# One Strassen product of the query projection split again into seven, and quadrant 3's value matmuls joined in both batches

## The chip, the core and the metric

The kernel runs on one core of a Trainium2 chip. A core has five engines with a queue of instructions each: TensorE (PE, matrix products, with its weight loads shown apart as PEld), VectorE (DVE), ScalarE (ACT), GpSimd (POOL) and SyncE (SP, which issues the DMAs). Matmuls write to PSUM, which DVE and ACT read; everything else lies in SBUF. The metric is the device time of the one core in microseconds (us), lower is better. The times shown are of executions without the profiler, except where "the profiled execution" is named.

## What is computed

`x` holds 64 batches of 128 tokens of 512 features. It is normalised, and goes through an attention with 16 query heads of 64 that share one key and one value head, with a bias per head and a causal and a key mask; the result is projected, normalised and added to `x`:

```python
xn = layernorm(x, g_in)
q = (xn @ Wq).reshape(b, n, H, DH).transpose(0, 2, 1, 3) * scale
k, v = split(xn @ Wkv)                     # one head; a null key and value in front
attn = softmax(q @ k^T + bias, masked)     # causal, and mask per key
out = (attn @ v).transpose(0, 2, 1, 3).reshape(b, n, INNER) @ Wo
return x + layernorm(out, g_out)
```

All is in 32-bit floats. `xn @ Wq` is 512 by 512 by 1024 for each group of four batches.

## The kernel before

**Tiles and loop.** The batches are worked on in groups of four (`GB`), and in steps `d` of two batches `a = 2d` and `b = 2d + 1`. A step is `turn(d)` followed by `body(d)`, for `d` from 1 to 29; `turn_end` and `body_end` do the last two, and a start-up part stands before. There is no scheduler: the order in which the functions issue their instructions is the order on each engine (`manual_schedule`), so whatever stands at the head of an engine's queue and waits holds up all that is behind it.

**A turn.** It issues the scores of batches `a` and `b` (L616), has DVE add them to bias and mask (L631, L633), and does the values of the pair before, `p = 2d - 2` and `p + 1` (`values`, L745). A values matmul uses 32 rows and 64 columns of the array. For each of four row quadrants `s` and two halves `r` a batch takes a matmul of 256 columns and three of 128; `wide` names quadrants in which two of those three, with the same weights, are joined into one of 256. Before the change quadrant 3 is joined in the first batch `p` of even steps, and nowhere else.

**The query projection.** For group `g = d//2 + 1`, one of the two halves `h = d % 2` of its features is made in a step. `[features x 512] @ [512 x tokens]` is done by Strassen's scheme (Winograd's form): seven products of half size instead of eight. `a11 ... a22` are quarters of `wq` (`a12`: the upper 256 input features, the lower half of the outputs), `s1, s2, s4, s3` sums of them made once, and `token_sum` makes four sums `xS` of the tokens on POOL, in even steps for both steps of a group. `product(g, f, k, ...)` (L539) is product `k` for output chunk `f` of 128: two matmuls of 128 by 128 weights and 256 columns. A step does chunks `f0 = 2h` and `f1 = 2h + 1`. Results collect in three kinds of PSUM tiles: "a" and "c", one buffer each, and "w", two buffers. `keep` copies a state of "a" to SBUF on ACT (`kp1`, `ku2`, `ku3`; one buffer for each name); `q_out` adds a PSUM tile and a kept one into the query tile `qT` on DVE (L560), or copies on ACT (L557). Product 5 opens a "c" tile and product 3 closes it; `q_out(.., "c", "u3")` reads it between these, and `q_out(.., "c", "u2")` after product 3. The next product 5 can open "c" only after that second read. Product 2 has a "w" tile for itself, and `q_out(g, f, 0, "w", "p1")` adds it to `kp1`.

**Order of a body on PE** (numbers are query products, of chunk f0, then f1; o1 ... o7 the output projection's products by the same scheme, L831): key and value products (L353), 1, 2, o1, 5, 6, o2, 7 of f0; 2 of f1; 4, 3 of f0; 1, 5 of f1; o5; 6 of f1; o6; 7; o3; 3; o7; 4; o4.

**Order on DVE between products 7 and 5:** `q_out(.., "c", "u3")`, the second batch's gain (`pair_gain`, L892) and residual (`pair_residual`, L895) of the output's normalisation, a transposition of new tokens (`tokens_T(m)`, L325), `q_out(.., "c", "u2")`, and the second `tokens_T`. The two transpositions are issued while there is a group after next (`xw`), up to step 27.

Of the kernel before, what the change touches and what calls it, by code (L numbers as in the profile page):

```python
# [8 lines left out]
FP = mybir.dt.float32  # L9
U8 = mybir.dt.uint8  # L10
AF = mybir.ActivationFunctionType
ALU = mybir.AluOpType
# [5 lines left out]
def kernel(  # L18
# [86 lines left out]
    const = ctx.enter_context(tc.tile_pool(name="const", bufs=1))  # L105
# [344 lines left out]
    xS, prod, kept = {}, {}, {}  # L450
# [11 lines left out]
    def q_part(g, c, h):  # L462

        return qT[g, c % NF, h][:, :, :, c // NF, :]
# [58 lines left out]
    def product(g, f, k, pool, tag, start=True):  # L523

        if start:
            prod[tag] = pool.tile([P, HT], FP, tag=tag, name=f"p{tag}_{g}_{f}_{k}")
        lo, hi = xT[g][:, 0 : GB // 2], xT[g][:, GB // 2 :]
        t1, t2, t3, t4 = (xS.get((g, i)) for i in range(1, 5))
        w, t = {
            1: (a11, lo[:, :, lo_k]),  # L530
            2: (a12, lo[:, :, hi_k]),
            3: (s4, hi[:, :, hi_k]),
            4: (a22, t4),
            5: (s1, t1),
            6: (s2, t2),
            7: (s3, t3),
        }[k]
        for kc in range(HK):
            nc.tensor.matmul(  # L539
                prod[tag],  # L540
                w[:, kc, f * P : (f + 1) * P],
                t[:, :, kc, :],
                start=(start and kc == 0),
                stop=(kc == HK - 1),
                skip_group_check=not start,
            )

    def keep(tag, name, slot=None):
        slot = slot or name
        kept[name] = bp.tile([P, HT], FP, tag=f"k{slot}", name=f"k{name}", bufs=1)  # L550
        nc.scalar.copy(kept[name], prod[tag])  # L551

    def q_out(g, c, h, tag, name=None):
        o = q_part(g, c, h)
        p = prod[tag].rearrange("p (t h i) -> p t h i", t=2, h=2)
        if name is None:
            nc.scalar.copy(o, p)  # L557
        else:
            k = kept.pop(name).rearrange("p (t h i) -> p t h i", t=2, h=2)
            nc.vector.tensor_tensor(o, p, k, ALU.add)  # L560


    S, nmax, rsum = {}, {}, {}

    def mask_neg(g):
# [159 lines left out]
    def values(b, wide=()):  # L725

        g, t = divmod(b, GB)
        sb = sbs.pop(b)
        po = pos[b]
        turns = (  # L730
            ((0, 0, 2), (1, 1, 1), (2, 1, 1), (3, 1, 1)),
            ((0, 0, 2), (1, 0, 1), (1, 1, 1), (2, 1, 1)),
        )
        for turn in range(len(turns[0])):
            for s in range(NQ):
                j, to, n = turns[s % 2][turn]
# [50 lines left out]
    P_LAST = B - 2  # L787
    lo_e, hi_e = slice(0, HE), slice(HE, DIM)
    lo_c, hi_c = slice(0, HC), slice(HC, NC)
    wT = const.tile([P, 4, HC, HE], FP, name="wT")  # L790
    e11, e12 = wo[:, lo_c, lo_e], wo[:, lo_c, hi_e]
    e21, e22 = wo[:, hi_c, lo_e], wo[:, hi_c, hi_e]
    yS = {}

    def out_weight_sum(k):
        p, m = ((e12, e11), (e22, wT[:, 0]), (e22, e12), (e21, wT[:, 1]))[k]
        nc.gpsimd.tensor_tensor(wT[:, k], p, m, ALU.subtract)

    def out_sum(p, k, eng=nc.gpsimd):

# [12 lines left out]
    def out_product(p, k, pool, tag, start=True):  # L813
        key = "y" + tag
        if start and pool is ps_s:
            two = ps_s.tile([P, 2, DIM], FP, tag="s", name=f"py_{p}_{k}_s")
            prod[key] = two[:, 0, 0:HE]
        elif start:
            prod[key] = pool.tile([P, HE], FP, tag=tag, name=f"py{tag}_{p}_{k}")
        a, b = oT[p], oT[p + 1]  # L820
        h, w = {
            1: (a[:, 0], e11),
            2: (a[:, 1], e21),
            3: (a[:, 1], e22),
            4: (b[:, 1], wT[:, 3]),
            5: (yS.get(p), wT[:, 0]),
            6: (a[:, 0], wT[:, 1]),
            7: (b[:, 0], wT[:, 2]),
        }[k]
        for c in range(HC):  # L830
            nc.tensor.matmul(  # L831
                prod[key],
                h[:, c, :],
                w[:, c, :],
                start=(start and c == 0),
                stop=(c == HC - 1),
                skip_group_check=not start,
            )
# [35 lines left out]
    def pair_pow(b):  # L874
        nc.gpsimd.tensor_tensor(yn[b][1], yn[b][1], nhalf, ALU.pow)
# [43 lines left out]
    def turn(d):  # L919

        a, b, p = 2 * d, 2 * d + 1, 2 * d - 2
        g = d // 2 + 1
        homes = (ps_y, "Y"), (ps_q, "a")
        if d == 1:
            homes = homes[::-1]
        scores(a, 0, (homes[0], (ps_w, "w")))
        scores(b, 0, (homes[1], (ps_w, "w")))
        scores(a, 1)
        scores(b, 1, ((ps_y, "X"), (ps_q, "c")))
        scores_add(a, 0)  # L930
        scores_add(b, 0)
        scores_max(a, 0)
        scores_add(a, 1)
        scores_add(b, 1)
        po = values_rooms(p)
        values(p, () if d % 2 else (3,))
        values(p + 1)
        if d % 2 and (d + 1) // 2 < NG:
            mask_neg((d + 1) // 2)
        bias_add(a + 2)  # L940
        if d % 2 == 0:
            token_sum(g, 1)
            token_sum(g, 2)
        exps(a, 0)
        values_out(p, po)
# [262 lines left out]
    def body(d):  # L1208
# [6 lines left out]
        m = (g + 1) * GB + 2 * h  # L1215
        sums = q and h == 0 and d > 0
        f0, f1 = 2 * h, 2 * h + 1

        if q:
            tags = [q_tags[g - 1, f, h] for f in range(NF)]  # L1220
# [6 lines left out]
        if ln:  # L1227
            pair_stats(l + 1)
            pair_pow(l + 1)
        if q:  # L1230
            kv_pair_out(g * GB + 2 * h, pkv)
            if h == 1:
                keys_T(g)
                values_spread(g)
# [12 lines left out]
            keep("a", "p1")  # L1247
        if ln:
            pair_norm(l)
        if q:  # L1250
            product(g, f0, 2, ps_w, "w")
            q_out(g, f0, 0, "w", "p1")
        if soft:
# [40 lines left out]
        if q:  # L1294
            product(g, f0, 7, ps_q, "a", start=False)
            keep("a", "u3")
            q_out(g, HC + f0, 1, "c", "u3")
        if ln:
            pair_gain(l + 1)
            pair_residual(l + 1)  # L1300
            store(l + 1)
# [2 lines left out]
            tokens_T(m)  # L1304
        if soft:
            exps(a, 1, 0, 1)
        if q:
            product(g, f1, 2, ps_w, "w")
            product(g, f0, 4, ps_q, "a", start=False)
            q_out(g, HC + f0, 0, "a")  # L1310
            product(g, f0, 3, ps_q, "c", start=False)
            q_out(g, f0, 1, "c", "u2")
# [14 lines left out]
        if q:  # L1327
            product(g, f1, 1, ps_q, "a")
            keep("a", "p1")
            q_out(g, f1, 0, "w", "p1")  # L1330
        if soft:
            exps(a, 1, 4)
# [10 lines left out]
        if q:  # L1343
            product(g, f1, 6, ps_q, "a", start=False)
            keep("a", "u2")
        if soft:
            exps(b, 1, 3)
            blocks_T(a)
# [29 lines left out]
        if out:  # L1378
            out_product(p, 4, ps_y, "X", start=False)
            out_part(p + 1, 0, "X")  # L1380

    def gains_T():
        pg = ps_y.tile([P, KC], FP, tag="X", name="pg")
# [177 lines left out]
```

## Time and profile before

| what | value |
|---|---|
| time, median of 3 executions | 1034.14 us (1033.25 to 1034.31) |
| the profiled execution's own time | 1033.72 us |
| its span, first to last instruction | 1031.9 us |
| two steps in the middle, 15 (odd, from 500.74 us) and 16 (even, from 532.19 us) | 31.45 and 31.48 us |

The profiled execution is one run of the program with the hardware profiler. Each matmul in 32-bit floats shows as two records on PE and two weight loads on PEld, so a product of two matmuls has four records. Rows of the timeline give the start in us, the time, the engine and line, the tiles (out<-in), the shape, the count of merged instructions, and in brackets the idle time before with what ended it. The duration of a record reaches to the end of its last write; the next instruction on the engine can start before that.

### The profile page before, as it was taken

How to read it: one execution, taken by the hardware profiler on the slowest of the kernel's cores; microseconds unless marked ns; L12 is line 12 of the kernel's file. 1: busy time of each engine (PE TensorE's matmuls, PEld its weight loads, DVE VectorE, ACT ScalarE, POOL GpSimd, SP SyncE). 2: the span in 40 equal slices, each digit the busy share in tenths (PEclk: the TensorE clock that was granted, in tenths of full speed). 3: DMA queues.
4: the chain of work that ended last, by engine and by line, in shares of the span. 5: the costliest groups of instructions: out<-in, count | busy, mean ns of one | idle time of the engine just before them, and what ended most of it. 6: DMA issues, size and time to landing. Idle time of an engine off the chain costs nothing.

```text
span 1031.9 us, 31175 instructions
## 1 busy us (share of the span) xinstructions
PE 1022.9 (99%) x12339; PEld 902.7 (87%) x12339; DVE 770.3 (75%) x1630; ACT 680.4 (66%) x2709; POOL 724.1 (70%) x537
## 2 busy tenths in 40 slices
PE   9999999999999999999999999999999999999997
PEld 8888888888888888888888888888888888888886
DVE  6877777876777877678777778777787777777597
ACT  4756667666677566686666776666776667856582
POOL 4997767676775867758667676676767677585676
PEclk9999999999999999999999999999999999999999
DMA  7514152241613325143151521415223161331311
GB/s 222 165 33 140 63 171 77 74 117 64 182 68 104 96 63 177 63 124 107 42 168 63 159 81 52 148 63 175 75 94 106 57 183 62 104 81 35 93 63 63
DMA packets 69226, 105.12 MB, mean 102 GB/s; under 512 B 9044, under 2 KB 33496, under 8 KB 67288
## 3 DMA queue, kind: packets, MB, share of 16 engines
q1 hardware_dynamic: 68784, 102.73, 31.8%
q8 instruction: 97, 1.59, 0.6%
q14 instruction: 49, 0.40, 0.1%
q10 hardware_dynamic: 296, 0.40, 0.1%
HBM read 67.45 MB, written 35.65 MB: 100 GB/s over the span
## 4 chain that ended last, share of the span: by engine, by line
PE 96%; DVE 2%; POOL 1%; issue 1%; DMA 0%; ACT 0%; POOLq 0%; DVEq 0%; ACTq 0%
PE pa L539 20%; PE pyX L831 19%; PE pyY L831 10%; PE pc L539 10%; PE po L745 7%; PE pkv L353 6%; PE pyw L831 5%; PE pw L539 5%; PE pq L474 3%; PE ps L616 3%; PE sc_X L616 2%; PE sc_Y L616 2%; PE py_s L831 1%; PE sc_a L616 1%; PE sc_w L616 1%; DVE sb L685 1%
## 5 line engine op out<-in xcount | busy, mean ns | idle before, releaser
L647 ACT ACTIVATE s<-s,nmax 128x65 f32<-128x65 f32 (+1 forms) x1024 | 372.0, 367 | 62.0 <-DVE nmax L638 62.0
L669 POOL TENSOR_TENSOR s<-s,rinv 128x512 f32<-128x512 f32 (+1 forms) x132 | 190.7, 1447 | 166.6 <-DVE rinv L665 166.6
L581 POOL TENSOR_TENSOR s<-biasp,mneg 128x1552 f32<-128x1552 f32 (+1 forms) x65 | 206.0, 3172 | 41.2 <-DVE s L631 32.8
L647 ACT ACTIVATION_READ_ACCUMULATOR s<-s,nmax 128x1 f32 x1024 | 194.3, 190 | 0.0
L831 PE MATMUL pyX<-wT,oT 128*128 128x256 f32 x696 | 164.4, 379 | 0.0
L685 DVE STREAM_TRANSPOSE sb<-s 128x1536 f32<-128x1536 f32 (+1 forms) x68 | 113.8, 1677 | 58.5 <-POOL s L669 58.5
L831 PEld LDWEIGHTS pyX<-wT,oT 128*128 128x128 f32 x696 | 132.1, 190 | 18.1
L638 DVE TENSOR_REDUCE nmax<-s 128x8 f32<-128x1032 f32 (+1 forms) x128 | 121.5, 950 | 0.1
L539 PE MATMUL pa<-xS,wq 128*128 128x256 f32 x472 | 121.2, 379 | 0.0
L557 ACT COPY qT<-pa 128x256 f32<-128x256 f32 x59 | 22.0, 373 | 147.1 <-PE pa L539 147.0
L539 PEld LDWEIGHTS pa<-xS,wq 128*128 128x128 f32 x472 | 89.4, 190 | 12.5 <-issue 0.2
L280 POOL TENSOR_TENSOR rstd<-rstd,nhalf 128x1 f32<-128x1 f32 x64 | 35.5, 555 | 74.1 <-DVE rstd L279 71.6
L811 POOL TENSOR_TENSOR oT<-oT 128x512 f32<-128x512 f32 x64 | 80.6, 1277 | 3.8 <-PE pyw L831 1.5
L745 PE MATMUL po<-sb,vr 32*64 32x256 f32 (+1 forms) x4008 | 81.8, 303 | 0.0
L745 PEld LDWEIGHTS po<-sb,vr 32*64 32x64 f32 x4008 | 71.4, 130 | 8.3 <-issue 5.7
L560 DVE TENSOR_TENSOR qT<-pc,ku 128x256 f32<-128x256 f32 x118 | 49.1, 416 | 39.5 <-ACT ku L551 22.4
L764 ACT ACTIVATE oT<-po,nv 128x512 f32<-128x512 f32 (+1 forms) x127 | 73.8, 656 | 0.2
L551 ACT COPY ku<-pa 128x256 f32<-128x256 f32 x118 | 43.9, 372 | 41.3 <-PE pa L539 38.1
L353 PE MATMUL pkv<-wkv,xT 128*128 128x128 f32 x512 | 65.6, 281 | 0.1
L353 PEld LDWEIGHTS pkv<-wkv,xT 128*128 128x128 f32 x512 | 59.7, 191 | 5.4 <-DVE s L631 4.8
L539 PE MATMUL pw<-xT,wq 128*128 128x256 f32 x240 | 61.4, 379 | 0.0
L539 PE MATMUL pa<-xT,wq 128*128 128x256 f32 x236 | 60.6, 379 | 0.0
(167 smaller groups left out, 2256.3 us busy)
## 6 DMA issues: line engine op xcount, KB each, us to landing
res<-in_x_dram SPq DMA_DIRECT2D x64, 256.0 KB, 2.9
x<-in_x_dram SPq DMA_DIRECT2D x63, 256.0 KB, 4.5
out_dram<-y SPq DMA_DIRECT2D x63, 256.0 KB, 2.3
xd<-xb SPq DMA_DIRECT2D x14, 1024.0 KB
xT<-xd SPq DMA_DIRECT2D x56, 256.0 KB, 5.9
vr<-vd SPq DMA_DIRECT2D x64, 128.0 KB, 2.7
kT<-kd SPq DMA_DIRECT2D x64, 64.0 KB, 2.1
wo<-in_L_cond_Wo_dram SPq DMA_DIRECT2D x1, 2048.0 KB, 13.5
```

Of the source, the lines that this page charges most:

```text
L353: nc.tensor.matmul(pkv, xT[g][:, t, kc, :], wkv[:, kc, :], start=(kc == 0), stop=(kc == KC - 1),)
L539: nc.tensor.matmul(prod[tag], w[:, kc, f * P : (f + 1) * P], t[:, :, kc, :], start=(start and kc == 0), stop=(kc == HK - 1), skip_group_ch ...
L581: nc.gpsimd.tensor_tensor(S[b][:, :, keys], biasp[:, :, keys], mneg[:, t, keys] .unsqueeze(1) .broadcast_to([P, R8, keys.stop - keys.start ...
L616: nc.tensor.matmul(home[r][u * DH : (u + 1) * DH, f, :], qT[g, f, t // 2][rows, t % 2, hf, u], kT[g][rows, 0 : nk // Q, t, :], start=True, ...
L638: nc.vector.tensor_reduce(nmax[b][:, hf], S[b][:, :, WITH_NULL[hf]], AX.X, ALU.max, negate=True)
L647: nc.scalar.activation(row, row, AF.Exp, bias=nmax[b][:, hf, k : k + 1], accum_out=rsum[b][:, hf, k : k + 1],)
L669: nc.gpsimd.tensor_tensor(sv, sv, rinvs[b, hf][:, lo:hi].unsqueeze(2).broadcast_to([P, hi - lo, sv.shape[2]]), ALU.mult,)
L685: nc.vector.transpose(sbs[b][:, :, lo:hi].rearrange("p j e q -> p e j q"), S[b][:, lo:hi, 1 : ROW - 1].rearrange("p e (j k) -> p e j k", k=Q),
L745: nc.tensor.matmul(po[s][rows, to : to + n], vr[g][quad, j, t, :], sb[quad, slots, r * NF : (r + 1) * NF, :], start=(turn == 0), stop=True ...
L764: nc.scalar.activation(to, src, AF.Identity, bias=nv2)
L811: eng.tensor_tensor(o, a, b, op)
L831: nc.tensor.matmul(prod[key], h[:, c, :], w[:, c, :], start=(start and c == 0), stop=(c == HC - 1), skip_group_check=not start,)
```

## The change

- Product 2, `a12` times the upper features of the first two batches, is itself split into two by two by two blocks of 128 and done by the same scheme in seven matmuls of 128 columns (`inner_product`), for both chunks `f0` and `f1` together, where before there were two for f0 and two for f1, of 256 columns. This holds for steps 2 to 29 (`deep`); step 1 goes as before.
- The seven lie in one "w" tile with four places of 128 columns. Matmul 1 stands where product 2 of f0 stood; 6, 5 and 2 stand after product 7 of f0; product 2 of f1, which came next, is gone; 7 stands after product 1 of f1; 4 and 3 after product 6 of f1.
- Two additions of 256 columns on DVE (`q_out(.., "w", "p1")`) become seven of 128 (`inner_out`). One stands where the first stood; two stand around `q_out(g, HC + f0, 1, "c", "u3")`; two where the second stood; two before `blocks_T(a)`.
- POOL makes the token sums (`token_sums_inner`, three subtractions of 256, 128 and 128 columns) in even steps after `pair_pow(l + 1)`. DVE makes the weight sums (`weight_sums_inner`, four of 256 columns) once, at the end of step 1.
- Quadrant 3's values are joined in both batches of every step from 2 on.
- For room, the output projection's third weight sum replaces `e12` in place, so that `wT` has three parts instead of four; one warm-up matmul is dropped (`keep_busy(7)`).

```diff
+    wL = const.tile([P, 3, 2, P], FP, name="wL")
+    in_four = a12.rearrange("p k (h f m) -> p k f h m", h=2, f=2)
+    d11, d12 = in_four[:, 0, 0], in_four[:, 1, 0]
+    d21, d22 = in_four[:, 0, 1], in_four[:, 1, 1]
+    r1, r2, r4 = (wL[:, i] for i in range(3))
+    r3 = d21
+    def weight_sums_inner():
+        for o, p, m, op in (
+            (r1, d21, d22, ALU.add),
+            (r2, r1, d11, ALU.subtract),
+            (r4, d12, r2, ALU.subtract),
+            (r3, d11, d21, ALU.subtract),
+        ):
+            nc.vector.tensor_tensor(o, p, m, op)
+    def token_sums_inner(g):
+        x = gp.tile([P, 4, N], FP, tag="xL", name=f"xL_{g}", bufs=1)
+        lo = xT[g][:, 0 : GB // 2]
+        nc.gpsimd.tensor_tensor(x[:, 0:2], lo[:, 1, hi_k], lo[:, :, HK], ALU.subtract)
+        nc.gpsimd.tensor_tensor(x[:, 2], lo[:, 1, KC - 1], x[:, 0], ALU.subtract)
+        nc.gpsimd.tensor_tensor(x[:, 3], lo[:, 0, KC - 1], x[:, 2], ALU.subtract)
+        xL[g] = x
+    def inner_product(g, h, k):
+        if k == 1:
+            inner[g, h] = ps_w.tile([P, 4, N], FP, tag="w", name=f"pl_{g}_{h}")
...
+        w, t, at = {
+            1: (d11, lo[:, 0, HK], 0),
+            2: (d12, lo[:, 0, KC - 1], 2),
+            3: (r4, lo[:, 1, KC - 1], 1),
+            4: (d22, t4, 0),
+            5: (r1, t1, 1),
+            6: (r2, t2, 0),
+            7: (r3, t3, 0),
+        }[k]
+        nc.tensor.matmul(
+            inner[g, h][:, at],
+            w[:, h],
+            t,
+            start=k == 1,
+            stop=True,
+            skip_group_check=k != 1,
+        )
+    def inner_out(g, h, f, t, at, name=None):
+        o = q_part(g, 2 * h + f, 0)[:, t]
+        p = inner[g, h][:, at].rearrange("p (h i) -> p h i", h=2)
+        k = o
+        if name is not None:
+            k = kept[name].rearrange("p (t h i) -> p t h i", t=2, h=2)[:, t]
+        nc.vector.tensor_tensor(o, p, k, ALU.add)
...
-        values(p, () if d % 2 else (3,))
-        values(p + 1)
+        values(p, () if d == 1 else (3,))
+        values(p + 1, () if d == 1 else (3,))
...
+        deep = q and d > 1
...
+        if sums:
+            token_sums_inner(g)
...
-        if q:
+        if deep:
+            inner_product(g, h, 1)
+            inner_out(g, h, 0, 0, 0, "p1")
+        elif q:
             product(g, f0, 2, ps_w, "w")
             q_out(g, f0, 0, "w", "p1")
...
         if q:
             product(g, f0, 7, ps_q, "a", start=False)
             keep("a", "u3")
+        if deep:
+            for k in (6, 5, 2):
+                inner_product(g, h, k)
+            inner_out(g, h, 0, 1, 0, "p1")
+        if q:
             q_out(g, HC + f0, 1, "c", "u3")
+        if deep:
+            inner_out(g, h, 0, 0, 2)
...
+        if q and not deep:
+            product(g, f1, 2, ps_w, "w")
         if q:
-            product(g, f1, 2, ps_w, "w")
             product(g, f0, 4, ps_q, "a", start=False)
             q_out(g, HC + f0, 0, "a")
             product(g, f0, 3, ps_q, "c", start=False)
             q_out(g, f0, 1, "c", "u2")
...
             product(g, f1, 1, ps_q, "a")
             keep("a", "p1")
+        if deep:
+            inner_product(g, h, 7)
+            inner_out(g, h, 1, 1, 0, "p1")
+            inner_out(g, h, 1, 1, 1)
+        elif q:
             q_out(g, f1, 0, "w", "p1")
...
             product(g, f1, 6, ps_q, "a", start=False)
             keep("a", "u2")
+        if deep:
+            inner_product(g, h, 4)
+            inner_product(g, h, 3)
+            inner_out(g, h, 1, 0, 0, "p1")
+            inner_out(g, h, 0, 1, 1)
...
+        if d == 1:
+            weight_sums_inner()
...
-    keep_busy(8)
+    keep_busy(7)
```

More of the change, by code (lines that the diff above doesn't have):

```diff
@@ L560, in q_out @@
             nc.vector.tensor_tensor(o, p, k, ALU.add)
+    wL = const.tile([P, 3, 2, P], FP, name="wL")
[4 more added lines that the diff above has]
+    r3 = d21
+    xL, inner = {}, {}
+    def weight_sums_inner():
[16 more added lines that the diff above has]
+            inner[g, h] = ps_w.tile([P, 4, N], FP, tag="w", name=f"pl_{g}_{h}")
+        lo = xT[g][:, 0 : GB // 2]
+        x = xL.get(g)
+        t1, t3, t2, t4 = (x if x is None else x[:, i] for i in range(4))
+        w, t, at = {
[22 more added lines that the diff above has]
+        nc.vector.tensor_tensor(o, p, k, ALU.add)
     S, nmax, rsum = {}, {}, {}
@@ L789 @@
     lo_c, hi_c = slice(0, HC), slice(HC, NC)
-    wT = const.tile([P, 4, HC, HE], FP, name="wT")
+    wT = const.tile([P, 3, HC, HE], FP, name="wT")
     e11, e12 = wo[:, lo_c, lo_e], wo[:, lo_c, hi_e]
     e21, e22 = wo[:, hi_c, lo_e], wo[:, hi_c, hi_e]
+    sums_e = wT[:, 0], wT[:, 1], e12, wT[:, 2]
     yS = {}
     def out_weight_sum(k):
-        p, m = ((e12, e11), (e22, wT[:, 0]), (e22, e12), (e21, wT[:, 1]))[k]
-        nc.gpsimd.tensor_tensor(wT[:, k], p, m, ALU.subtract)
+        p, m = ((e12, e11), (e22, sums_e[0]), (e22, e12), (e21, sums_e[1]))[k]
+        nc.gpsimd.tensor_tensor(sums_e[k], p, m, ALU.subtract)
     def out_sum(p, k, eng=nc.gpsimd):
@@ L824, in out_product @@
             3: (a[:, 1], e22),
[L825 to L828, printed above, removed]
+            4: (b[:, 1], sums_e[3]),
+            5: (yS.get(p), sums_e[0]),
+            6: (a[:, 0], sums_e[1]),
+            7: (b[:, 0], sums_e[2]),
         }[k]
```

## The prediction

> **What bounds the kernel now.** I read the page first: busy shares, and the chain that ended last.
>
> ```profile
> PE 1022.9 (99%) x12339; PEld 902.7 (87%) x12339; DVE 770.3 (75%) x1630; ACT 680.4 (66%) x2709; POOL 724.1 (70%) x537
> PE 96%; DVE 2%; POOL 1%; issue 1%; DMA 0%; ACT 0%; POOLq 0%; DVEq 0%; ACTq 0%
> ```
>
> PE is never without work. So matmul time taken out is a gain only if nothing else becomes late, and any wait that PE gets is a loss. Next the stage table, for steps 15 and 16 (span, then busy time of PE, PEld, DVE, ACT, POOL):
>
> ```profile
> 500.74:532.19 31.45, 31.45 (x386) 27.78 (x385) 23.86 (x51) 21.75 (x85) 19.71 (x15) 1.00 0.48 140
> 532.19:563.67 31.48, 31.48 (x382) 27.80 (x381) 23.52 (x50) 20.72 (x83) 24.02 (x18) 1.00 0.19 66
> ```
>
> Averages hide where DVE is tight, so I went through step 15 in the timeline, PE first:
>
> ```profile
> 506.03 2.05 PE L353 MATMUL pkv<-wkv,xT 128*128 128x128 f32 x16
> 507.92 1.03 PE L539 MATMUL pa<-xT,wq 128*128 128x256 f32 x4
> 508.79 1.03 PE L539 MATMUL pw<-xT,wq 128*128 128x256 f32 x4
> 509.65 1.89 PE L831 MATMUL pyX<-wo,oT 128*128 128x256 f32 x8
> 511.38 1.03 PE L539 MATMUL pc<-xS,wS 128*128 128x256 f32 x4
> 512.24 1.03 PE L539 MATMUL pa<-xS,wS 128*128 128x256 f32 x4
> 513.10 1.89 PE L831 MATMUL pyw<-wo,oT 128*128 128x256 f32 x8
> 514.83 1.03 PE L539 MATMUL pa<-xS,wq 128*128 128x256 f32 x4
> 515.69 1.03 PE L539 MATMUL pw<-xT,wq 128*128 128x256 f32 x4
> 516.56 1.03 PE L539 MATMUL pa<-xS,wq 128*128 128x256 f32 x4
> 517.42 1.03 PE L539 MATMUL pc<-xT,wS 128*128 128x256 f32 x4
> 518.28 1.03 PE L539 MATMUL pa<-xT,wq 128*128 128x256 f32 x4
> 519.15 1.03 PE L539 MATMUL pc<-xS,wS 128*128 128x256 f32 x4
> ```
>
> These are, from 507.92: products 1 and 2 of f0, o1, 5, 6, o2, 7 of f0 (514.83), 2 of f1 (515.69), 4 and 3 of f0, then 1 (518.28) and 5 (519.15) of f1. A product starts 0.863 us after the one before, 0.216 a record. The place to look at is product 5 of f1, which opens a new "c" tile. Weight loads, DVE and ACT around it:
>
> ```profile
> 517.21 0.84 PEld L539 LDWEIGHTS pc<-xT,wS 128*128 128x128 f32 x4
> 518.07 0.84 PEld L539 LDWEIGHTS pa<-xT,wq 128*128 128x128 f32 x4
> 519.03 0.73 PEld L539 LDWEIGHTS pc<-xS,wS 128*128 128x128 f32 x4
> ```
> ```profile
> 515.45 0.37 DVE L861 TENSOR_TENSOR y<-pyw,kyp 128x256 f32<-128x256 f32 x1
> 516.30 0.42 DVE L560 TENSOR_TENSOR qT<-pc,ku 128x256 f32<-128x256 f32 x1 [0.47 <-ACT ku L551]
> 516.64 0.69 DVE L892 TENSOR_TENSOR yn<-yn,gob 128x512 f32<-128x512 f32 x1
> 517.36 0.69 DVE L895 TENSOR_TENSOR y<-yn,res 128x512 f32<-128x512 f32 x1
> 517.97 0.70 DVE L325 STREAM_TRANSPOSE xb<-x 128x512 f32<-128x512 f32 x1
> 518.60 0.39 DVE L560 TENSOR_TENSOR qT<-pc,ku 128x256 f32<-128x256 f32 x1
> ```
> ```profile
> 515.89 0.37 ACT L551 COPY ku<-pa 128x256 f32<-128x256 f32 x1 [0.84 <-PE pa L539]
> ```
>
> Weight loads come 0.86 apart (517.21, 518.07), so the next was due at 518.93; it came at 519.03, 0.04 after the second `q_out` from "c" ended on DVE (518.60 + 0.39 = 518.99). The matmul followed at 519.15, just on time. **This hand-over has no slack left**, though no idle time shows. The chain behind it: product 7 of f0, ACT's copy, `q_out(.., "c", "u3")` at 516.30, gain, residual and transposition without a gap, `q_out(.., "c", "u2")` at 518.60: 2.30 us from the first `q_out` to the second.
>
> **The change part by part.** The rows for small matmuls and small additions:
>
> ```profile
> L353 PE MATMUL pkv<-wkv,xT 128*128 128x128 f32 x512 | 65.6, 281 | 0.1
> L399 DVE TENSOR_TENSOR kvt<-pkv,nkv 128x256 f32<-128x256 f32 x31 | 13.2, 424 | 19.1 <-PE pkv L353 19.1
> L388 DVE TENSOR_TENSOR kvt<-pkv,nkv 128x128 f32<-128x128 f32 x2 | 0.5, 281 | 0.0
> ```
>
> *Matmuls.* The key and value products, 16 records of 128 columns, take from 506.03 to 507.92: 1.89 us, 0.118 a record, more than half of 0.216. Seven inner matmuls are 14 records, 1.65 us; the four taken out are 1.73. By itself that saves 0.075 us a step, 2.1 us in 28 steps. The shape is the same as in that row, so I take it; at half of 0.216 a record the saving would be 0.215 a step, 6.0 in all.
>
> [...]
>
> *Where PE then stands.* Matmul 1 (0.236) in place of product 2 of f0 brings all that follows forward by 0.627: product 7 of f0 to 514.20. Matmuls 6, 5, 2 (0.708) follow from 515.07 to 515.77. Products 4, 3 of f0 and 1 of f1 (2.59) and matmul 7 (0.236) follow, and product 5 of f1 is due at 518.60, 0.55 earlier than now. Matmuls 4 and 3 (0.472) come behind it.
>
> *Where DVE then stands.* In the built program `inner_out(g, h, 0, 1, 0, "p1")` stands ahead of `q_out(.., "c", "u3")` and waits for the third of matmuls 6, 5, 2. Its last record starts at 515.65 and ends 0.28 later, 515.93; DVE follows a PE group by 0.04:
>
> ```profile
> 508.12 0.42 DVE L399 TENSOR_TENSOR kvt<-pkv,nkv 128x256 f32<-128x256 f32 x1 [0.59 <-PE pkv L353]
> ```
>
> (that group ended at 506.03 + 2.05 = 508.08). So it starts at 515.97, when DVE has long done the addition at 515.45. Additions of 256 columns start 0.34 apart (516.30 to 516.64) at a duration of 0.42; one of 128 is 0.14 shorter by the rows above (424 and 281), so 0.20 apart. Then: `inner_out` 0.20, `q_out` 0.34, the second `inner_out` 0.20, gain, residual and transposition 1.96 (516.64 to 518.60): the second `q_out` starts at 518.67, ends at 519.06, and the matmul follows 0.16 after that (518.99 to 519.15): **519.22**. PE was due at 518.60: it waits 0.62 us, with 0.05 of that taken earlier at product 4 (ACT's copy) and 0.13 at product 3 (which needs the first `q_out`), all inside the same total. Behind product 5 nothing is shorter, and matmuls 4 and 3 add 0.472. So a step grows by 0.07 + 0.47 = **0.54 us**, instead of shrinking by 0.075.
>
> [...]
>
> Bounds for the price of 128 columns in DVE's queue: 0.34 each, the same as 256 (+0.28 on the chain), or nothing (then the second `q_out` starts at 518.27 and PE still waits 0.22, a step growing by 0.14). I take 0.20, from the nearest row.
>
> The wait repeats while the transposition stands in the chain: steps 2 to 27, 26 times, 14.0 us. In steps 28 and 29 the chain is shorter by 0.63 and I count the saving of 0.075 each.
>
> *Values.* Value stages without a join (step 15) and with one (step 16):
>
> ```profile
> 503.58:506.03 2.45, 2.45 (x128) 2.20 (x128) 1.00 0.03 7
> 535.03:537.51 2.48, 2.48 (x124) 2.23 (x124) 1.00 0.21 78
> ```
>
> The one with a join has four records fewer and takes 0.03 us longer. No row shows both batches joined. Bounds per step: as much again for each (+0.06 odd, +0.03 even), or a gain of the mean share of the records left out (8 of 128 in 2.45: 0.15). I take 2.48 for both: +0.4 us in all; bounds -3.8 to +1.3.
>
> *The rest.* POOL's token sums:
>
> ```profile
> 535.06 1.27 POOL L521 TENSOR_TENSOR xS<-xT 128x512 f32<-128x512 f32 x1
> 541.35 0.55 POOL L280 TENSOR_TENSOR rstd<-rstd,nhalf 128x1 f32<-128x1 f32 x1 [1.70 <-DVE rstd L279]
> ```
>
> 512 columns take 1.27, so 512 in three pieces some 1.7 us, and they stand in POOL's idle 1.70 before 541.35: nothing. The inner weight sums, once:
>
> ```profile
> 89.56 1.77 DVE L685 STREAM_TRANSPOSE sb<-s 128x1536 f32<-128x1536 f32 x1
> 92.47 0.42 DVE L631 TENSOR_TENSOR s<-sc_w,s 128x256 f32<-128x256 f32 x1 [1.13 <-PE sc_w L616]
> L507 DVE TENSOR_TENSOR wS<-wq 128x1024 f32<-128x1024 f32 x1 | 1.3, 1314 | 0.0
> ```
>
> A quarter of 1.3 each, four times, 1.3 us after the transposition, against 1.13 idle: 0 to 1 us once; I take 0.3. The warm-up matmul dropped: nothing, at most two records of 0.118 either way.
>
> **Sum.** 14.0 - 0.15 + 0.4 + 0.3 = 14.6 us on the profiled execution's 1033.72 (span 1031.9): 1048.3. That execution is 0.4 below the median of 1034.14, so 1048.7 beside the median.
>
> **Rivals.** (1) *Faster, no wait in its place.* If DVE came to the second `q_out` 0.62 us earlier than I work out, PE would keep the 2.1 us, and up to 6.0 with records at half price: 1028 to 1032. It decides at product 5 of f1: there DVE must be done by 518.55 in step 15's time. For it: DVE is idle 25% of the time and other hand-overs have room. Against: that idle time lies elsewhere; even free additions leave a wait of 0.22. [...] (2) *A smaller wait:* small additions nearly free, or joined values gaining their 0.15: 26 times 0.14 and the 0.5 above give 1038, with the values 1036. (3) *A larger one:* small additions at 0.34, or the late DVE making more waits behind (`blocks_T(a)` has two additions ahead of it now): 26 times 0.28 or 7.3 more, 1056. (4) *The change doesn't act:* the built program has the seven matmuls and the 60 value matmuls per step; under 0.01.
>
> **How the numbers follow.** 0.2% of 1034 is 2 us, about what a measurement of this kernel tells from no change. Forecast 0.75, rival 2 0.10, rival 3 0.06, rival 1 with a gain over 2 us 0.06, within 2 us 0.03. Range: the additions at 0.13 to 0.27 give 3.6 either way, the values -3.8 to +1.3, DVE's hand-over times 0.02 a step or 0.5: 1041 to 1054. That leaves 0.25 out, so the lower end goes to 1038, into rival 2. Faster 0.06, same 0.03, slower 0.91.
>
> **What would show it.** Right: steps 2 to 27 last about 32.0 us; the four records of product 5 of f1 start late, with PEld or PE idle before them on DVE's addition into qT; the DVE queue has no gap from the first inner addition after product 7 to the second `q_out`; steps 28 and 29 are at 31.4 or so. Wrong: if product 5 starts at once, or if a step's time is under 31.45; if the 14 records take other than 1.65; if value stages differ from 2.48.

## The result, and the profile after

The changed kernel takes **1052.28 us** (median of 6, 1051.84 to 1052.82), the kernel before 1034.07 (median of 6, 1033.25 to 1034.31): a ratio of 1.0178, with a 95% interval of 1.0165 to 1.0191, or 18.2 us more. The prediction was 1048.7 in a range of 1038 to 1054, slower.

The page of the changed kernel shows the loss where it was expected, with DVE in the chain of work that ended last (9%, where it had 2%):

```profile
PE 1029.7 (98%) x12337; PEld 908.4 (87%) x12337; DVE 795.2 (76%) x1774; ACT 678.2 (65%) x2709; POOL 745.5 (71%) x579
PE 88%; DVE 9%; issue 1%; POOL 1%; DMA 0%; POOLq 0%; DVEq 0%
```

The table by stretches of the changed kernel gives step 2, step 15 and step 29 (length, busy time and count of PE, PEld, DVE, ACT, POOL, then the granted clock of TensorE, DMA share, GB/s):

```profile
91.54:130.28 38.74, 33.82 (x383) 29.51 (x383) 30.13 (x58) 20.78 (x83) 25.95 (x21) 0.91 0.15 53
513.38:545.31 31.93, 31.69 (x384) 27.97 (x383) 24.56 (x56) 21.67 (x85) 19.70 (x15) 1.00 0.47 139
959.83:991.25 31.42, 31.42 (x384) 27.89 (x383) 21.57 (x46) 20.25 (x83) 19.54 (x12) 1.00 0.29 85
```

Steps 3 to 27 all last 31.92 or 31.93 us, where they had 31.45 and 31.48: 25 times 0.46 is 11.5. Step 2 lasts 38.74 instead of 31.48: 7.3, once. Steps 28 and 29 last 31.42 each, where they had 31.59 and 31.82: 0.6 gained. The sum is 18.2; the spans (1050.0 and 1031.9) differ by 18.1. So there are **two losses**, and only the first was forecast.

**The loss in each step.** Step 15 of the changed kernel, in the timeline: first PEld, then PE, then DVE, from product 7 of f0 to product 5 of f1.

```profile
528.33 0.73 PEld L539 LDWEIGHTS pa<-xS,wq 128*128 128x128 f32 x4
529.25 0.73 PEld L539 LDWEIGHTS pc<-xT,wS 128*128 128x128 f32 x4 [0.19 <-DVE qT L560]
...
531.71 0.73 PEld L539 LDWEIGHTS pc<-xS,wS 128*128 128x128 f32 x4 [0.43 <-DVE qT L560]
```
```profile
527.71 0.61 PE L605 MATMUL pl<-xL,wL 128*128 128x128 f32 x4
528.15 0.39 PE L605 MATMUL pl<-xT,wq 128*128 128x128 f32 x2
528.38 1.09 PE L539 MATMUL pa<-xS,wq 128*128 128x256 f32 x4
529.30 1.08 PE L539 MATMUL pc<-xT,wS 128*128 128x256 f32 x4
530.22 1.03 PE L539 MATMUL pa<-xT,wq 128*128 128x256 f32 x4
531.09 0.38 PE L605 MATMUL pl<-xL,wq 128*128 128x128 f32 x2
531.71 1.13 PE L539 MATMUL pc<-xS,wS 128*128 128x256 f32 x4 [0.24 <-DVE qT L560]
532.68 1.89 PE L892 MATMUL pyY<-wT,yS 128*128 128x256 f32 x8
```
```profile
528.58 0.29 DVE L621 TENSOR_TENSOR qT<-pl,kp 128x128 f32<-128x128 f32 x1 [0.23 <-PE pl L605]
528.78 0.41 DVE L560 TENSOR_TENSOR qT<-pc,ku 128x256 f32<-128x256 f32 x1
529.11 0.28 DVE L621 TENSOR_TENSOR qT<-pl,qT 128x128 f32<-128x128 f32 x1
529.31 0.69 DVE L953 TENSOR_TENSOR yn<-yn,gob 128x512 f32<-128x512 f32 x1
530.04 0.69 DVE L956 TENSOR_TENSOR y<-yn,res 128x512 f32<-128x512 f32 x1
530.64 0.70 DVE L325 STREAM_TRANSPOSE xb<-x 128x512 f32<-128x512 f32 x1
531.27 0.39 DVE L560 TENSOR_TENSOR qT<-pc,ku 128x256 f32<-128x256 f32 x1
```

DVE has no gap from the inner addition at 528.58 to the second `q_out` at 531.27, which ends at 531.66; the weight load of product 5 starts at 531.71. Without a wait the matmul would have come at 531.31 (531.09 and two records of 0.11). It starts 0.40 later and goes on 0.10 more slowly than usual (0.97 to the next group, not 0.863): 0.51. Product 4 takes 0.06 more (528.38 to 529.30) and product 3 as well (529.30 to 530.22). The three waits together are 0.63. The view of waits adds the whole run up (total us, times, longest us):

```profile
PEld pc L539 <- DVE qT L560: 13.9, 40, 0.4
PE pc L539 <- DVE qT L560: 6.2, 26, 0.2
```

26 times on PE: one for each of the steps 2 to 27.

**The loss in step 2.** The same view of the changed kernel at the end of step 1 and the start of step 2, DVE, then POOL, then PE; the last fence gives the value stage by the table of stretches.

```profile
91.09 0.38 DVE L578 TENSOR_TENSOR wL<-wq 128x256 f32<-128x256 f32 x1
91.51 3.35 DVE L578 TENSOR_TENSOR wL<-wL,wq 128x256 f32<-128x256 f32 x1
94.89 1.37 DVE L578 TENSOR_TENSOR wL<-wq,wL 128x256 f32<-128x256 f32 x1
96.18 1.48 DVE L578 TENSOR_TENSOR wq<-wq 128x256 f32<-128x256 f32 x1
97.58 0.41 DVE L691 TENSOR_TENSOR s<-sc_w,s 128x256 f32<-128x256 f32 x1
```
```profile
91.25 3.33 POOL L641 TENSOR_TENSOR s<-biasp,mneg 128x1552 f32<-128x1552 f32 x1 [0.48 <-DVE sb L745]
94.53 1.45 POOL L521 TENSOR_TENSOR xS<-xT 128x512 f32<-128x512 f32 x1
96.06 1.32 POOL L521 TENSOR_TENSOR xS<-xT,xS 128x512 f32<-128x512 f32 x1
```
```profile
99.14 4.57 PE L805 MATMUL po<-sb,vr 32*64 32x256 f32 x120 [4.68 <-DVE s L691]
```
```profile
99.14:103.64 4.50, 4.50 (x121) 3.68 (x121) 4.38 (x9) 2.77 (x16) 0.93 (x1) 0.50 0.02 4
```

The four weight sums are all of one size. The first takes 0.38 us; the next three take 3.35, 1.37 and 1.48, and end 0.3 or less after a POOL instruction that was already running does (94.58, 95.98, 97.38). So the score additions of step 2 start at 97.58, and PE stands idle for 4.68 us. It pays twice: after the idle time the granted clock is 0.50, and the value stage takes 4.5 us where it has 2.47 in other steps. 4.7, 2.0 and the 0.5 of every step make up the 7.3.

### The profile page after: what moved, and what is told of

It is laid out like the page before. It is cut to its first block, busy times and chain, and to the rows that moved or that the text cites. A ratio compares the mean times of both kernels' runs of the same rounds, so it can differ in the third digit from the quotient of the medians.

```text
span 1050.0 us, 31371 instructions
## 1 busy us (share of the span) xinstructions
PE 1029.7 (98%) x12337; PEld 908.4 (87%) x12337; DVE 795.2 (76%) x1774; ACT 678.2 (65%) x2709; POOL 745.5 (71%) x579
## 3 DMA queue, kind: packets, MB, share of 16 engines
q8 instruction: 97, 1.59, 0.6%
## 4 chain that ended last, share of the span: by engine, by line
PE 88%; DVE 9%; issue 1%; POOL 1%; DMA 0%; POOLq 0%; DVEq 0%
PE pyX L892 19%; PE pa L539 15%; PE pyY L892 10%; PE pc L539 8%; PE po L805 7%; PE pkv L353 6%; PE pyw L892 5%; PE pl L605 4%; PE pq L474 3%; PE ps L676 3%; PE sc_X L676 2%; DVE qT L560 2%; DVE y L956 2%; DVE yn L953 2%; DVE xb L325 2%; PE sc_Y L676 1%
## 5 line engine op out<-in xcount | busy, mean ns | idle before, releaser
L892 PE MATMUL pyX<-wo,oT 128*128 128x256 f32 x464 | 109.7, 379 | 0.0
L892 PE MATMUL pyX<-wT,oT 128*128 128x256 f32 x464 | 109.7, 379 | 0.0
L539 PEld LDWEIGHTS pa<-xS,wq 128*128 128x128 f32 x472 | 87.3, 190 | 11.5 <-issue 0.2
L892 PEld LDWEIGHTS pyX<-wo,oT 128*128 128x128 f32 x464 | 86.0, 190 | 10.5
L892 PEld LDWEIGHTS pyX<-wT,oT 128*128 128x128 f32 x464 | 85.9, 190 | 10.7
L621 DVE TENSOR_TENSOR qT<-pl,kp 128x128 f32<-128x128 f32 x112 | 31.3, 280 | 82.2 <-PE pl L605 80.9
L805 PE MATMUL po<-sb,vr 32*64 32x128 f32 (+1 forms) x3840 | 83.6, 316 | 4.7 <-DVE s L691 4.7
L539 PE MATMUL pc<-xS,wS 128*128 128x256 f32 x236 | 63.3, 390 | 6.2 <-DVE qT L560 6.2
```

The source lines that it names most:

```text
L539: nc.tensor.matmul(prod[tag], w[:, kc, f * P : (f + 1) * P], t[:, :, kc, :], start=(start and kc == 0), stop=(kc == HK - 1), skip_group_ch ...
L805: nc.tensor.matmul(po[s][rows, to : to + n], vr[g][quad, j, t, :], sb[quad, slots, r * NF : (r + 1) * NF, :], start=(turn == 0), stop=True ...
L892: nc.tensor.matmul(prod[key], h[:, c, :], w[:, c, :], start=(start and c == 0), stop=(c == HC - 1), skip_group_check=not start,)
```

## The experiments

Theories: (A) the loss per step is the wait of product 5 for DVE's second `q_out`, as predicted; (B) the loss in step 2 is the weight sums held up by POOL; rivals are named in each expectation. All ratios are against the kernel before, run on the same chip.

### The second read ahead of the transposition

The changed kernel with one line moved: `q_out(g, f0, 1, "c", "u2")` goes ahead of `tokens_T(m)`.

```diff
-            tokens_T(m)
...
             product(g, f0, 3, ps_q, "c", start=False)
             q_out(g, f0, 1, "c", "u2")
         if xw:
+            tokens_T(m)
             tokens_T(m + 1)
```

> The changed kernel with the second read of the c tile (q_out of u2) issued on DVE ahead of both transpositions of tokens instead of between them. Theory (the c tile's second read, held up behind the transposition, is what product 5 of f1 waits for): the 0.51 us that this product loses goes in steps 2 to 27, 13 us in all, so 1039 us, steps of 31.4. Rival A (the small matmuls and their weight loads cost PE the time, and DVE's reads only show it): no change, 1052. Rival B (DVE is short of time all through the step): the wait comes up again at another tile, 1045 to 1052.

Measured: 1038.8, ratio 1.0047 (1.0032 to 1.0062). Steps 3 to 29 last 31.42. In its timeline of step 15, DVE and then PEld, the read now ends at 525.16; the last load below, of product 5, follows the one before it without a wait; of the loads shown only the first, of product 3, still has one:

```profile
524.75 0.41 DVE L560 TENSOR_TENSOR qT<-pc,ku 128x256 f32<-128x256 f32 x1
```
```profile
523.36 0.73 PEld L539 LDWEIGHTS pc<-xT,wS 128*128 128x128 f32 x4 [0.19 <-DVE qT L560]
...
524.97 0.41 PEld L605 LDWEIGHTS pl<-xL,wq 128*128 128x128 f32 x2
525.30 0.73 PEld L539 LDWEIGHTS pc<-xS,wS 128*128 128x128 f32 x4
```

Theory A is shown: 13.5 us of the 18.2 hang on the place of one read in DVE's queue.

### One small DVE addition more, and nothing else of the change

The kernel before, with one addition of 128 columns behind the first `q_out`. Its result is used by nothing.

```diff
             q_out(g, HC + f0, 1, "c", "u3")
+            if d > 1:
+                nc.vector.tensor_tensor(spare, prod["c"][:, 0:N], ident, ALU.add)
```

> The kernel before, with one more addition of 128 columns on DVE (the c tile's first half plus the identity, into a spare tile) between the first read of the c tile and the gain, in steps 2 to 29; nothing else of the change. It adds nothing to the output. Theory (the hand-over of the c tile to product 5 of f1 has no slack): steps 2 to 27 grow by the 0.20 us that the addition takes in the queue, 5.2 us, 1039.3. Rival (the hand-over has room and PE's small matmuls make the loss): 1034.1, no change.

Measured: 1038.9, ratio 1.0048 (1.0031 to 1.0064). Most steps last 31.67 and 31.64, which is 0.19 more than before, although the matmuls are the same. Its DVE queue shows the price of 128 columns directly, 0.20 from start to start:

```profile
519.20 0.28 DVE L1300 TENSOR_TENSOR spare<-pc,ident 128x128 f32<-128x128 f32 x1
519.40 0.69 DVE L893 TENSOR_TENSOR yn<-yn,gob 128x512 f32<-128x512 f32 x1
```

So the hand-over had no slack, as read from the profile of before: 0.20 on DVE came out as 0.19 on the end, in an engine that is idle a quarter of the time.

### The weight sums on POOL

The changed kernel with `nc.gpsimd` for `nc.vector` in `weight_sums_inner`.

> The changed kernel with the four inner weight sums, made once at the end of step 1, issued on POOL instead of DVE, at the same place. Theory (DVE's additions with both inputs in SBUF wait there for POOL's long additions, and the turn of step 2 waits for DVE): the 7.2 us by which step 2 is longer go, less up to 3 us by which POOL's bias additions come later: 1045 to 1048. Rival (step 2 is long for another reason, such as the first use of the inner tiles or late tokens): 1052, step 2 still 38.7.

Measured: 1046.19, ratio 1.0118 (1.0103 to 1.0134). Step 2 lasts 32.90, the later ones 31.92 as in the changed kernel. Step 2 gives 5.8 of the 6.1 us that this kernel is faster than the changed one. It is still 1.0 longer than the steps behind it: the four sums now stand ahead of POOL's next bias addition; that this is the cause was not tried.

### The weight sums on DVE while POOL is idle

The changed kernel with `weight_sums_inner()` moved from the end of step 1 to the place ahead of `rinv(a, 1)` in step 1. Same instructions, same engine.

```diff
             exps(a, 1, 4)
+            if d == 1:
+                weight_sums_inner()
             rinv(a, 1)
...
-        if d == 1:
-            weight_sums_inner()
```

> The changed kernel with the four inner weight sums still on DVE, but issued in step 1 ahead of the reciprocal for batch a, where POOL has nothing to do. Theory (they are slow only because POOL works at the same time): 0.3 to 0.55 us each, step 2 no longer than the others, 1045 us. Rival (these additions take 1.4 to 3.4 us by themselves, for instance by their strides): they hold up the reciprocal and all behind it, 1049 to 1052.

Measured: 1045.55, ratio 1.0111 (1.0096 to 1.0126). Step 2 lasts 31.92. DVE's timeline of this kernel; POOL has nothing between 79.00 and 82.02:

```profile
80.16 0.41 DVE L578 TENSOR_TENSOR wL<-wq 128x256 f32<-128x256 f32 x1
80.61 0.42 DVE L578 TENSOR_TENSOR wL<-wL,wq 128x256 f32<-128x256 f32 x1
81.07 0.42 DVE L578 TENSOR_TENSOR wL<-wq,wL 128x256 f32<-128x256 f32 x1
81.41 0.42 DVE L578 TENSOR_TENSOR wq<-wq 128x256 f32<-128x256 f32 x1
```

Theory B is shown: the additions that took 3.35, 1.37 and 1.48 beside POOL take 0.42 without it.

### Both mended, and one step further

The changed kernel with both moves (the second read first, the sums while POOL is idle):

> The changed kernel with both cures: the second read of the c tile ahead of the transpositions, and the inner weight sums on DVE in step 1 where POOL is idle. Theory (the two causes are apart and add): 1052.3 less 13.5 less 6.7, 1032.1; steps 2 to 29 of 31.42, which still hold two short waits of PE, 0.06 us each, at products 4 and 3 of f0. Rival (one cure takes part of the other's gain, or a new wait comes up): 1034 to 1039.

Measured: 1032.38, ratio 0.9984 (0.9975 to 0.9993); steps of 31.42. The same with `q_out(g, HC + f0, 1, "c", "u3")` moved ahead of the inner addition in front of it as well:

> As the one with both cures, and the first read of the c tile (q_out of u3) also goes ahead of the inner addition that waits for matmuls 6, 5 and 2. Theory (product 3's 0.06 us, and no other, comes from that read standing behind the inner addition): steps of 31.36, 1030.4. If ACT's copy holds product 4 as before, its 0.06 stays. Rival (the reads' order is worth nothing once the second is early): 1032.1, as without it.

Measured: **1031.61**, ratio 0.9976 (0.9967 to 0.9986); steps of 31.42 and 31.36 by turns. It is the fastest version found. The expected 31.36 came in the odd steps only: there product 3's 0.06 is gone, and product 4's stays. In the even ones product 3 had no wait; there some 0.12 stands at product 4 (in step 16 of this kernel it starts 0.27 after matmul 2, and product 3 0.94 after it), and stays. The gain of both parts of the change together is clear of the noise, but small: 0.05 to 0.09 us a step in steps 2 to 27, 1.9 us in all. The other 0.5 us come from steps 28 and 29, which the kernel before lost to something else (see theory C).

### The join alone, and the change without the join

The kernel before with quadrant 3 joined in both batches from step 2 on:

> The kernel before, with quadrant 3's values joined in both batches of every step from 2 on; no inner products. Theory (the join is worth nothing, since the value stage was seen at 2.466 us with both joined, between 2.451 without and 2.479 with one): 1034.1 within 0.5. Rival (the join gives back what is left out, 84 matmuls): 1031 to 1033.

Measured: 1038.8, ratio 1.0042 (1.0029 to 1.0054). Then the fastest version with the joins as they were before the change:

> The kernel with both reads first, and quadrant 3's values joined as before the change: only in the first batch of even steps. Theory (the join is worth nothing): as that kernel, within 0.5 us, 1030.4. Rival (a join in both batches gains where PE has nothing else to wait for): 1 to 3 us above it.

Measured: 1037.78, ratio 1.0032 (1.0021 to 1.0042). **Both expectations failed**, and in opposite senses: adding the join to the one kernel costs 4.8 us, taking it from the other costs 6.2. So the price is not that of the joined matmul. In both kernels the steps have become irregular, 31.4 to 32.3, and value stages (in one step the key and value products behind one) are broken up by idle time for which the profile names no releaser. The weight loads of a value stage of before, of the join alone, and of the version without the join:

```profile
912.61 2.31 PEld L745 LDWEIGHTS po<-sb,vr 32*64 32x64 f32 x124 [0.17 <-issue]
```
```profile
126.28 0.63 PEld L745 LDWEIGHTS po<-sb,vr 32*64 32x64 f32 x22 [0.17 <-issue]
127.53 1.84 PEld L745 LDWEIGHTS po<-sb,vr 32*64 32x64 f32 x98 [0.62 <-issue]
```
```profile
820.79 2.27 PEld L805 LDWEIGHTS po<-sb,vr 32*64 32x64 f32 x127 [0.17 <-issue]
823.69 0.13 PEld L805 LDWEIGHTS po<-sb,vr 32*64 32x64 f32 x1 [0.63 <-issue]
```

What the two share is that the number of instructions per step has changed. Each record is one weight load and one matmul. Before, a step has 384 records (odd) or 380 (even); the changed kernel has 382 in each, because the join takes out 8 or 4 and the inner matmuls add 6. The join alone has 376, the version without the join 390 and 386. With its sequencer's few, TensorE has 1538 instructions in two steps before the change and after it, 1514 in the join alone and 1562 without the join. The profile of before has a DMA queue for instructions, with 97 packets:

```profile
q8 instruction: 97, 1.59, 0.6%
```

1.59 MB in 97 packets is 16.4 KB each; and PE and PEld of before have 2 times 12339 instructions, 254 for each packet, or 256 with the 188 of TensorE's sequencer. The page has 95 packets for the 12171 records of the join alone and 98 for the 12505 of the version without it, so it is TensorE's instructions that they carry. So theory C: these are fetched in blocks of 16 KB, 256 of them or 128 records, three blocks to a step. 1538 is six blocks and 2 instructions, so the edges of the blocks fall at nearly the same place in each step; with 1514 or 1562 they wander, and where an edge falls inside the value stage, whose 120 to 128 records last only 2.45 to 2.48 us, PE runs dry. That the changed kernel kept the number of before was luck.

### Theory C: the count kept, and the start shifted

The join in both batches again, but with quadrant 0's first matmul split in two in as many batches as the join was added to, so that the count is again 384 and 380:

```diff
-        values(p, () if d % 2 else (3,))
-        values(p + 1)
+        values(p, () if d == 1 else (3,), (0,) if d > 1 and d % 2 else ())
+        values(p + 1, () if d == 1 else (3,), () if d == 1 else (0,))
```

> The kernel before, with quadrant 3 joined in both batches of each step from step 2, as in the join alone; but the first matmul of quadrant 0 is split into two halves in as many batches as the join is added to, so that each step issues as many matmuls as before (384 and 380 records, where the join alone has 376 in every step). Theory: the join as such is nearly free, and what made it slow is that TensorE's instructions are fetched in blocks of 16 KB, three to a step, and that the place in the step where a fetch falls drifts when a step no longer issues three blocks' worth; the count kept, the steps stay at 31.45 to 31.50 us each and the time at 1034 to 1035. Rival: the joined matmul itself costs (a read of longer strides, or the values' result later); then 1038.8 as in the join alone, with irregular steps.

Measured: 1037.66, ratio 1.0033 (1.0021 to 1.0046). The steps are regular again, 31.55 and 31.58 by turns from step 2 to 22 (one is 31.61), and no value stage has a break. But the time is not the expected one, since the split has a price that the expectation left out: the value stages of steps 15 and 16 last 2.58 (four matmuls split) and 2.55 (two), where the changed kernel's, joined in both batches and unsplit, last 2.47. The weight loads of the one in step 15, from 505.18 to the first load behind it:

```profile
505.18 2.41 PEld L750 LDWEIGHTS po<-sb,vr 32*64 32x64 f32 x128 [0.17 <-issue]
507.76 1.86 PEld L353 LDWEIGHTS pkv<-wkv,xT 128*128 128x128 f32 x16 [0.17 <-issue]
```

So this run supports the count and leaves its total to the split (0.10 a step, 2.8 us in 28 steps) and to four late steps of 0.3 to 0.4 more, whose wait lies at the key and value products.

The next three are the kernel before with more matmuls in the second warm-up, and nothing else. They move the edges in all later steps alike.

```diff
-    keep_busy(5)
+    keep_busy(5 + 64)      # or 57, or 32
```

> The kernel before with 64 matmuls more in the second warm-up, which are 128 records and 256 instructions of TensorE: one whole block of the fetch. By the fetch theory every later fetch falls where it fell before: steps as before, 31.45 and 31.48 us, and only the start is longer, by at most 128 records of 0.115 us = 14.7 us: 1049. A theory without a fetch gives the same; this run is the control for the next two.

Measured: 1047.73, ratio 1.0133 (1.0118 to 1.0148). Step 2 starts 14.8 us later than before, and steps 2 to 22 last 31.48 and 31.45 as before; of the seven behind them the odd ones go up to 31.62, where before had 31.59 and 31.82 in its last two.

> The kernel before with 57 matmuls more in the second warm-up: 228 instructions, 28 short of a block, so every later fetch comes 28 instructions later in the step than before. The join alone was 24 to 36 instructions late in its steps from 123 to 188 us and lost 0.36 to 0.6 us in each, so by the fetch theory the start is 13.1 us longer and 27 steps lose 0.3 to 0.6 us each: 1055 to 1063, more than with 64, though it does less. Rival (the place of a fetch costs nothing): steps as before, and 1.6 us less than with 64, 1047.2.

Measured: 1050.74, ratio 1.0160 (1.0145 to 1.0175). Seven matmuls fewer than in the run above, and 3.0 us slower: step 2 starts 2.4 us earlier, and steps 2 to 29 lose 5.0 us, up to 0.78 in one. The total lies between what the theory and the rival had expected.

> The kernel before with 32 matmuls more in the second warm-up: 128 instructions, half a block. The join alone was as far out of place around 440 us and lost 0.1 to 0.2 us per step there; by the fetch theory the start is 7.4 us longer and 27 steps lose some 0.12 us each: 1044 to 1046. Rival (the place of a fetch costs nothing): 1041.5.

Measured: 1048.2, ratio 1.0136 (1.0120 to 1.0151). Half as many as in the first, and no faster: 8.0 us of start are saved and 7.5 lost in the steps, more than either side had expected. The weight loads of a bad value stage with 57 more, then with 32 more:

```profile
835.37 0.62 PEld L745 LDWEIGHTS po<-sb,vr 32*64 32x64 f32 x21 [0.17 <-issue]
836.63 1.79 PEld L745 LDWEIGHTS po<-sb,vr 32*64 32x64 f32 x107 [0.64 <-issue]
```
```profile
926.08 1.36 PEld L745 LDWEIGHTS po<-sb,vr 32*64 32x64 f32 x69 [0.17 <-issue]
927.76 1.10 PEld L745 LDWEIGHTS po<-sb,vr 32*64 32x64 f32 x55 [0.32 <-issue]
```

With 57 more the break comes after 21 records, with 32 more after 69: 48 records later for 25 matmuls, or 50 records, fewer in front. So the break has its place in the instruction stream and not in the work, and with a whole block in front (64) steps 2 to 22 last as before.

That it is the fetch that PE waits for can be read from the traces by counting. Take the weight loads, matmuls and sequencer's instructions of TensorE in front of a break, and the end of the packet of the instruction queue that has the number of that block (the 89th packet for 89 x 256):

| run | break ends, us | instructions in front | after its packet's end, us |
|---|---|---|---|
| join alone | 127.53 | 10 x 256 + 193 | 1.42 |
| without the join | 823.69 | 78 x 256 + 193 | 1.32 |
| 57 more | 836.63 | 77 x 256 + 193 | 1.40 |
| 32 more | 927.76 | 86 x 256 + 194 | 1.23 |
| count kept, a late step | 761.52 | 71 x 256 + 193 | 1.51 |
| before, its step 29 | 947.58 | 89 x 256 + 193 | 1.24 |

All 39 breaks of 0.2 us or more that have no named releaser, inside the value stages and the key and value products of steps 2 to 29 in the 14 traces (the two kernels and the twelve runs), are at 193 or 194 of 256 and end 1.2 to 1.6 us after their packet. Nowhere in the 14 traces does the first load of a block start sooner than 1.17 us after its packet. The time that PE loses at these places is 4.9 us in the join alone, 5.6 in the version without the join, 5.2 and 8.0 with 57 and 32 more, and 1.7 with the count kept, against 0.8 in the kernel before and 0.3 in the fastest version: to within 0.6 us the whole loss of their steps. So theory C is shown, for the late steps of the run with the count kept too. What stays open is what sets the start of a packet, and with it why a broken step loses now 0.1, now 0.8, and why the expected sizes (0.3 to 0.6 a step with 57, 0.12 with 32) came out as 0.18 and 0.27.

## Why the prediction was right, point by point

- **The wait at product 5.** Right in place, cause and size. Expected was a wait of 0.62 in all, 0.05 of it at product 4 and 0.13 at product 3; in step 15 it is 0.63, with 0.06 at each and 0.51 at product 5. From the first `q_out` to the second DVE takes 2.49 (528.78 to 531.27), as worked out: 0.34 + 0.20 + 1.96. Moving the second read took away the loss.
- **The 14 records.** Mis-sized. Matmuls 6, 5 and 2 take 0.67 for six records (527.71 to 528.38), 0.111 each and not 0.118: 1.55 us for 14, a saving of 0.17 a step. The row of the key and value products, 0.118 a record, was too dear for them by 6%. It made little difference, since DVE sets the time of product 5: up to the group after it a step grew by 0.03 and not 0.07 (532.68 is 19.30 into its step; in before it was 19.27), and matmuls 4 and 3 add 0.44 and not 0.47.
- **Steps 28 and 29.** They gain 0.17 and 0.40, not 0.075 each. Of that, 0.11 and 0.37 are waits of the kernel before at its key and value products, at the start of a block of instructions (theory C), by which its steps 28 and 29 last 31.59 and 31.82 where the others have 31.48 and 31.45; the changed kernel does not have them. The change itself saves 0.06 and 0.03 there: about 0.17 by the records, less waits of some 0.12 at products 4 and 3 that the prediction had not put into these two steps.
- **Values joined in both batches.** 2.48 was taken, 2.467 came. Right as a duration. But the step "the mean share of the records left out, or as much again" looked for the join's price inside the value stage alone; joins also set how many instructions a step has, and by what the fastest version lost, the change would have been some 6 us slower without them (an estimate; that kernel was not run). The rival with joined values gaining 0.15 is out.
- **The inner weight sums.** The step that failed: "0 to 1 us once; I take 0.3", with the sum of 1.3 us taken from one row of 1024 columns. It was 6.8 (38.74 less 31.92). The bound was wrong because only DVE's own queue was looked at, and neither POOL's instruction in the same time nor what a late score addition does to PE. The profile of before already held the warning. The first fence below is DVE, the second POOL: the row of 1.3 us had POOL beside it, and there POOL took longer (2.25 against 1.27 in the row that the prediction shows for the same addition); the next sum of the same size took 2.18, as did the third, and the fourth 2.11. The prediction took the cheapest of the four.

```profile
40.16 1.31 DVE L507 TENSOR_TENSOR wS<-wq 128x1024 f32<-128x1024 f32 x1
41.51 2.18 DVE L507 TENSOR_TENSOR wS<-wS,wq 128x1024 f32<-128x1024 f32 x1
```
```profile
40.35 2.25 POOL L521 TENSOR_TENSOR xS<-xT 128x512 f32<-128x512 f32 x1
```

- **Why POOL matters there.** The runs show it for these sums, which have both inputs in SBUF: 3.35 beside POOL's 3.33, 0.42 with POOL idle. The other additions of a step have one input in PSUM, and in the changed kernel none is held up: 55 of the 56 residual additions run beside POOL, and each of the 56 takes 0.69. (`yn`, their first input, lies in PSUM, where ACT writes it; the text ahead of the prediction has only matmuls writing there.) Those of 256 columns take 0.43 at most, beside POOL or not.
- **The sum.** 14.6 forecast, 18.2 measured: 2.9 too much for the steps (14.0 − 0.15 + 0.4 = 14.3, against 26 times 0.46 less 0.6 in the last two, 11.4), and 6.5 too little for the weight sums. The range held because its upper end had been set for other unknowns, by luck as far as the sums go.
- **The rivals.** "Faster, no wait in its place" was held to decide at product 5 of f1 with DVE done by some 0.6 us sooner. That is what the moved read does, and with the sums moved too the time is 1032.38, just past the slow end of that rival's 1028 to 1032. The point of decision was right; the gain was smaller than its lower end, since product 4 and product 3 keep their waits, some 0.12 a step. By the prediction's own 0.16 from the end of DVE's addition to the matmul, DVE had to be done by 518.44 there and not 518.55. Rival 2's 1036 does not follow from its own terms either: with the values at -3.8 its sum is 1034.

## What to carry to other kernels

In front of a tile that is about to be opened again, put the read that frees it ahead of everything in that engine's queue that nobody waits for; here the place of one such read was worth 13.5 us in all, and one addition of 0.20 us ahead of it cost 0.19 us a step, on an engine that is idle a quarter of the time. Price a DVE instruction with both inputs in SBUF by what POOL does at that time, not by its duration alone: three of the weight sums here took 3.35, 1.37 and 1.48 us beside POOL and 0.42 without. And when an edit changes the number of matmuls in a step by a few, look whether the steps are still all alike before the edit itself is blamed or praised: with 1514 or 1562 instructions of TensorE in two steps instead of 1538 they lasted 31.4 to 32.3 us.

## What the runs showed of the hardware that was not expected

- TensorE's instructions came in blocks of 16 KB (97 packets for 1.59 MB in the kernel before, 256 instructions for each), and the 39 breaks counted above stand at 193 or 194 of 256. In no trace of this case does a block's first weight load start sooner than 1.17 us after its packet's end, and where the edge of a block fell in a dense stage a step lost 0.1 to 0.8 us by it: the version without the join, with less than 2% of the matmuls changed, is 6.2 us slower than the fastest version, and PE loses 5.6 us at these places. In the kernel before, with three edges to a step too, steps 2 to 27 last 31.45 to 31.48 us; a step with a break at an edge, its step 29, lasts 31.82.
- After 4.7 us without work PE's granted clock was 0.50 over the value stage that followed, which took 4.50 us and not 2.47: with the idle time, 6.7 us in step 2.
- Value matmuls of 256 columns split into two cost 0.08 us for two of them and 0.11 for four (2.550 and 2.579 against 2.467, with four and eight records more), while joining two of 128 with the same weights gains next to nothing (2.451 unjoined, 2.479 joined in one batch, 2.467 in both).
